# A graph attention layer on one core: target loads cut in 96 and 15 rows, weights moved to the second node pass, gather buffers from five to six

## The chip, the core and the metric

The kernel runs on one core of one Trainium2 chip. The metric is the time of one execution on the device, in microseconds (us). The core has five engines that run their own instruction streams and wait for each other by semaphores: TensorE (PE in the profile, with PEld for its weight loads), VectorE (DVE), ScalarE (ACT), GpSimd (POOL) and SyncE (SP). SP issues most transfers, ScalarE a few, and POOL the indirect ones, which gather or scatter rows by a list of indices. Each of these queues issues in order.

## The reference

One layer of attention over a graph with N = 12500 nodes of 128 channels and E = 400000 edges, sorted by target node (`dst`).

```python
h = maximum(layernorm(x), 0)
msg_src, msg_dst = h @ w_src + b_src, h @ w_dst          # per node
m = (msg_src[src] + msg_dst[dst]) * edge_weight * mlp(edge_attr)   # per edge; mlp 32-64-64-128, silu
m = m @ w_sep + b_sep                                    # 8 heads of 16 alphas and 16 values
score = sum(leaky(alpha) * alpha_dot)                    # leaky: a smooth leaky relu
att = softmax of score over the edges of one target
out = x + segment_sum(value * att, dst) @ w_proj + b_proj
```

## The kernel before

**Node passes** (in `gnn_kernel`, lines 171 to 618). The 98 blocks of up to 128 nodes go in 25 quads of four. The first pass (loop at line 575) does for each quad i: transposes of the normalized quad i + 1 and their relu (`turn`), the scaling of quad i + 3 on ScalarE and VectorE (`norm`), the product with w_src (`products(i, 0)`), whose result ScalarE copies to one of six buffers `ms0` and SP stores to the table `t_src` in memory, and the statistics of quad i + 5 (`stats`, `roots`, `scales`). The second pass (line 605) multiplies the same quads, kept in SBUF, with w_dst and stores pairs of quads to `t_dst` through four buffers `ms1`. It also normalizes 40 tiles of raw rows that POOL gathered for the first five steps (`raw_norm`, `raw_turn`), and runs a list of single jobs (`extra`).

Beside the passes lies work on the sorted targets. `load_targets` brings dst into the tile `cur`, 112 rows of seven sections of 512 edges; 111 rows are full and are loaded at once, the last one alone, and single words fill the columns at both sides. `load_limits` brings single words that are compared with thresholds. `sections` takes the first and last target of each section, `falls` and `fits` test whether the input has the expected shape and set `bad`, which decides a branch ahead of `windows`. `fits` ends with the stores of the sections' borders to memory (`ends_d`) and loads them back in three layouts (`eb`, `base`, `to`). In the first pass SP also issues the 29 loads of small weights and four of edge attributes, two a quad from quad 3 on (`weights_list`). `marks`, `spans`, `cuts`, `places`, `direct_ids` and `spreads` prepare, during the second pass, what the steps need; `cuts` and `places` alternate between TensorE and VectorE.

**Steps** (in `windows`, `step(k)`, line 1508). 391 steps of two sections (1024 edges) follow. Step k = 5 and later gather their source rows from `t_src` in eight indirect transfers of 128 rows (`gather`, line 1036), issued by POOL; steps 5 to 12 into the ring `messages`, later ones into the buffers `gs0` and `gs1`, one for each section of a step, GSB = 5 of each. TensorE turns them (`sources`, line 1096), adds the target rows (`message`, line 1108), VectorE multiplies with the radial network's result (`radial`, line 1085, which takes the edge weights from `w_b`). Then come alphas, scores, the softmax over eight steps at once (`softmax_*`), and, LAG = 12 steps later, values and sums. SP's order in a step is written out: stores of the window sums, `load_w(k + 2)` (512 KB, edge weights sent to all partitions, three buffers), `load_md(k + 4)` (rows of `t_dst`), every second step `load_d` (targets, `d_b`), then the later stores.

**Tail.** After the last step POOL loads rows of x into gather buffers (`big["xw"]`, `big["xe"]`) and the finished block rows from `obs_d` into two of the `w_b` buffers (`big["ye"]`), adds them (`sum_rows`) and scatters them to the output.

The pool `node` (h, ms0, ms1) is opened ahead of `node1` (x_all, cur, eb and others); the pools of `windows` take the same space afterwards, `lp` (loads) from its right end and `sp` (work tiles) from its left.

Of the kernel before, what the change touches and what calls it, by code (L numbers as in the profile page):

```python
# [21 lines left out]
P = 128  # L22
C = 128
# [28 lines left out]
GSB = 5  # L52
# [3 lines left out]
def gnn_kernel(ctx: ExitStack, tc: tile.TileContext, a: dict, out: bass.AP):  # L56
# [45 lines left out]
    groups = [(max(t, 0), min(t + XG, NF)) for t in range(4 - XG, NF, XG)]  # L102
# [69 lines left out]
    with tc.tile_pool(name="node", bufs=2) as np_, tc.tile_pool(name="node1", bufs=1) as n1, \  # L172
# [6 lines left out]
        nc.scalar.dma_start(out=w_dst, in_=a["w_dst"])  # L179
# [17 lines left out]
        assert 96 <= CP - 1 < P and 0 < CL < CC  # L197
        ones_b = n1.tile([P, 1], BF16, name="ones_b")
# [49 lines left out]
        def weights_list():  # L248

            pairs = []  # L250
            for name, t in wt.items():
# [149 lines left out]
        def fits():  # L401
# [11 lines left out]
            for n, o0, o1 in ((CP, 0, CL), (CP - 1, CL, CC)):  # L413
                for o in range(o0, o1, BANK):
# [18 lines left out]
            nc.vector.tensor_copy(bad, sum_)  # L433
            e0 = 1 + 2 * (CP - 1) * SPP
            nc.sync.dma_start(out=ends_d[:, 1:e0].rearrange("o (p c) -> (o p) c", p=CP - 1),
                              in_=ends[0:CP - 1].rearrange("p s i -> p (s i)"))
# [5 lines left out]
            nc.sync.dma_start(out=t_dst[N:N + W, :], in_=bare[:W, 0:C])  # L442
            nc.sync.dma_start(out=eb.rearrange("p s i -> p (s i)"),
# [20 lines left out]

        def places():

            on = n1.tile([NC, P], F32, name="on")
            nc.vector.tensor_tensor(on, to[:, 0, :], to[:, 1, :], op=ALU.is_equal)
            nc.vector.scalar_tensor_tensor(on, on, SKIP, to[:, 0, :], op0=ALU.mult, op1=ALU.add)
            pt = nps.tile([P, NC], F32, name="pb", bufs=1)  # L470
            nc.tensor.transpose(pt, on, ident[:NC, :NC])
            nc.vector.tensor_copy(ids, pt)
# [62 lines left out]
        def marks(j):  # L535
            s_ = slice(j * CC // 4, (j + 1) * CC // 4)
            nc.vector.tensor_tensor(sm[:, s_], cur[:, s_], cur[:, s_.start + 1:s_.stop + 1], op=ALU.not_equal)
            if j == 3:
                h = (CP - 1) * CC
                nc.sync.dma_start(out=same[:, 0:h].rearrange("o (p c) -> (o p) c", c=CC), in_=sm[0:CP - 1, :])  # L540
# [25 lines left out]
        for i in range(2, 5):  # L566
            stats(*quads[i])
            if i == 2:
                roots(*quads[i])
                scales(*quads[i])  # L570
                norm(i)
        ready = quads[3][0], quads[4][1]
        roots(*ready)
        more = iter(weights_list())
        for i in range(Q):
            if i + 1 < Q:
                turn(i + 1)
            if ready:
                scales(*ready)
                ready = None  # L580
# [3 lines left out]
            if i + 5 < Q:  # L584
                stats(*quads[i + 5])
            if i % 2 and i + 4 < Q:
                ready = quads[i + 4][0], quads[min(i + 5, Q - 1)][1]
                roots(*ready)
            if i == 1:
                load_targets()  # L590
                load_limits()
            if i >= 3:
                for load in (next(more, None), next(more, None)):
                    if load:
                        load()
# [8 lines left out]
        assert 2 * RQ + 1 < Q  # L604
        for i in range(Q):
            if i % 2 and 0 <= i // 2 - 1 < RQ:
                raw_turn(i // 2 - 1)
            products(i, 1)
            if i % 4 == 0 and i // 2 < RQ:
                raw_roots(i // 2, i // 2 + 2)  # L610
# [4 lines left out]
            if i in extra:  # L615
                extra[i]()
            if i == 2 * RQ - 2:
# [313 lines left out]
    def windows():  # L931
# [7 lines left out]
        with tc.tile_pool(name="ps", bufs=1, space=PSUM) as pp, \  # L939
# [68 lines left out]
            def load_w(k):  # L1008
                w_g[k] = lp.tile([P, PR], F32, name="w_b", bufs=3)
# [481 lines left out]
            def ye_at(g):  # L1491
                return big["ye", g // 8][:, g % 8 * C:(g % 8 + 1) * C]
# [10 lines left out]
            load_d(0)  # L1503
            for k in range(2):
                load_md(k)
                load_w(k)

            def step(k):
# [10 lines left out]
                if has(k + 2) and k >= 0:  # L1519
                    load_w(k + 2)  # L1520
# [138 lines left out]
            g0 = min(8, last - 1)  # L1659
            nc.gpsimd.dma_start(out=big["ye", 0][:, 0:g0 * C].rearrange("p (g c) -> p g c", c=C),  # L1660
                                in_=obs_d[0:g0 * P, :].rearrange("(g p) c -> p g c", p=P))
# [205 lines left out]
```

## Time and profile before

| | before |
|---|---|
| median of 3 runs | 4101.05 us (4093.68 to 4102.66) |
| profiled execution | 4092.9 us |
| its span | 4091.1 us |
| granted TensorE clock, mean | 0.987 |
| second node pass ends, steps begin | about 128 us |
| last gather of a step issued | 3988 us |

A page of the profile tells of one execution: busy time of each engine, the transfers, the chain of work that ended last, and the costliest groups of instructions by line. Views of the trace answer for a stretch of time, one line or one engine. In a row of the timeline stand start, duration, engine, line, operation, and in brackets the engine's idle time before it and what ended it. In a row of the waits stand the waiting line, what it waited for, the total, the count and the longest. In a row of busy time by stretch stand the stretch, then the busy time of PE, PEld, DVE, ACT and POOL with their counts (or of one line alone), the granted clock, the share of the DMA engines that was busy, and GB/s. "SPq" marks instructions of SP that issue transfers.

### The profile page before, as it was taken

How to read it: one execution, taken by the hardware profiler on the slowest of the kernel's cores; microseconds unless marked ns; L12 is line 12 of the kernel's file. 1: busy time of each engine (PE TensorE's matmuls, PEld its weight loads, DVE VectorE, ACT ScalarE, POOL GpSimd, SP SyncE). 2: the span in 40 equal slices, each digit the busy share in tenths (PEclk: the TensorE clock that was granted, in tenths of full speed). 3: DMA queues.
4: the chain of work that ended last, by engine and by line, in shares of the span. 5: the costliest groups of instructions: out<-in, count | busy, mean ns of one | idle time of the engine just before them, and what ended most of it. 6: DMA issues, size and time to landing. Idle time of an engine off the chain costs nothing.

```text
span 4091.1 us, 84238 instructions
## 1 busy us (share of the span) xinstructions
PE 3864.8 (94%) x27816; PEld 2340.9 (57%) x27816; DVE 3107.1 (76%) x5569; ACT 1880.1 (46%) x3824; POOL 3036.2 (74%) x3199
## 2 busy tenths in 40 slices
PE   6799999999999999999999999999999999999996
PEld 5455655655555555555555555555555555555555
DVE  6577777777777777777778777787777777777777
ACT  5454444444444444444444444444444444444441
POOL 4757777777777777777777777777777777777776
PEclk8899999999999999999999999999999999999998
DMA  6767777777767776776777676777776777767662
GB/s 212 216 172 196 195 179 194 195 179 194 197 185 178 193 192 170 190 196 182 179 191 195 190 188 188 187 184 192 200 194 177 192 199 193 189 187 196 187 174 56
DMA packets 534427, 762.19 MB, mean 186 GB/s; under 512 B 124496, under 2 KB 337522, under 8 KB 533871
## 3 DMA queue, kind: packets, MB, share of 16 engines
q1 hardware_dynamic: 375991, 498.26, 41.1%
q0 software_dynamic: 101872, 207.34, 23.3%
q10 hardware_dynamic: 56120, 51.10, 4.4%
q8 instruction: 226, 3.70, 0.4%
q14 instruction: 218, 1.79, 0.2%
HBM read 632.26 MB, written 125.70 MB: 185 GB/s over the span
## 4 chain that ended last, share of the span: by engine, by line
PE 62%; DMA 13%; POOL 10%; issue 7%; DVE 4%; ACT 2%; SPq 1%; ACTq 0%; DVEq 0%; POOLq 0%
PE V L1251 13%; PE pa L1119 12%; DMA gs<-t_src,idx 9%; POOL gs L1036 9%; PE misc L1264 7%; PE p L1080 6%; PE pm L1096 6%; PE m L1052 4%; PE pm L1108 4%; PE p L1065 3%; PE m L1136 3%; DVE mT L1113 1%; DMA agg<-ob 1%; DMA cur<-in_dst 1%; POOL mT L1036 0%
## 5 line engine op out<-in xcount | busy, mean ns | idle before, releaser
L1036 POOL DMA_INDIRECT gs<-t_src,idx x3021 | 2871.7, 951 | 942.1 <-issue 764.8
L1121 ACT ACTIVATE sl<-pa,c_b_a 128x512 f32<-128x512 f32 x782 | 537.4, 687 | 1087.8 <-PE pa L1119 1085.7
L1126 DVE SCALAR_TENSOR_TENSOR al<-pa,sl 128x512 f32<-128x512 f32 x782 | 537.6, 687 | 530.9 <-ACT sl L1121 522.6
L1251 PEld LDWEIGHTS V<-c_w_v,mT 128*128 128x128 f32 x6154 | 752.2, 192 | 304.8 <-DVE ob L1268 122.4
L1251 PE MATMUL V<-c_w_v,mT 128*128 128x128 f32 x6154 | 885.1, 287 | 2.8 <-DVE pvx L1253 2.7
L1119 PE MATMUL pa<-mT,c_w_a 128*128 128x512 f32 x1564 | 835.6, 616 | 25.0 <-DVE mT L1113 22.0
L1253 DVE TENSOR_TENSOR pvx<-V,Pem 128x512 f32<-128x512 f32 x770 | 529.2, 687 | 209.0 <-PE V L1251 190.7
L1067 ACT ACTIVATE h<-p,b 128x512 f32<-128x512 f32 x391 | 469.3, 1200 | 407.1 <-PE p L1065 328.8
L1096 PEld LDWEIGHTS pm<-ident,gs 128*128 128x128 f32 x3021 | 372.1, 141 | 483.7 <-issue 466.6
L1085 DVE SCALAR_TENSOR_TENSOR rad<-p,c_fc_b,w_b 128x1024 f32<-128x1024 f32 x391 | 501.1, 1281 | 108.0 <-PE p L1080 91.3
L1264 PEld LDWEIGHTS misc<-pvx,oh 128*64 128x64 f32 x6250 | 351.3, 137 | 292.2 <-ACT h L1055 281.9
L1096 PE MATMUL pm<-ident,gs 128*128 128x128 f32 x3021 | 456.4, 274 | 63.7 <-DMA gs<-t_src,idx 63.3
L1113 DVE SCALAR_TENSOR_TENSOR mT<-pm,c_b_src,rad 128x1024 f32<-128x1024 f32 x391 | 498.1, 1274 | 5.6 <-PE pm L1108 4.8
L1264 PE MATMUL misc<-pvx,oh 128*64 128x136 f32 x6250 | 450.9, 286 | 0.1
L1080 PE MATMUL p<-h,w3b 64*128 64x512 f32 x1564 | 405.1, 595 | 0.0
L1052 PE MATMUL m<-eT,w1b 64*128 64x256 f32 x782 | 275.7, 433 | 20.1 <-ACT qT L1346 14.2
L1108 PE MATMUL pm<-ohT,m 64*128 64x512 f32 x1564 | 286.7, 444 | 0.0
L1119 PEld LDWEIGHTS pa<-mT,c_w_a 128*128 128x128 f32 x1564 | 236.6, 191 | 75.5 <-DVE mT L1113 42.5
L1055 ACT ACTIVATE h<-misc,b 128x256 f32<-128x256 f32 x391 | 185.5, 474 | 201.5 <-PE misc L1052 184.1
L1052 PE MATMUL misc<-eT,w1b 64*128 64x256 f32 x782 | 275.8, 433 | 0.0
L1152 ACT ACTIVATE Sp<-m,b_s 128x512 f32<-128x512 f32 x192 | 131.7, 686 | 309.1 <-PE m L1136 306.8
L1065 PE MATMUL p<-h,w2b 64*64 64x256 f32 x3128 | 260.5, 403 | 2.7 <-DVE rad L1085 2.7
(217 smaller groups left out, 3552.5 us busy)
## 6 DMA issues: line engine op xcount, KB each, us to landing
w_b<-in_edge_weight SPq DMA_DIRECT2D x390, 512.0 KB
d_b<-in_dst SPq DMA_DIRECT2D x390, 256.0 KB
e_t<-in_edge_attr ACTq DMA_DIRECT2D x386, 128.0 KB
sc_d<-Sp SPq DMA_DIRECT2D x192, 256.0 KB
gs<-t_src,idx POOLq DMA_INDIRECT x3021
win<-ob SPq DMA_DIRECT2D x390, 68.0 KB
agg<-ob SPq DMA_DIRECT2D x762, 33.5 KB
md<-t_dst SPq DMA_DIRECT2D x782, 32.0 KB
```

The costliest lines, as they stand in the source:

```text
L1036: sent = [nc.gpsimd.indirect_dma_start(out=gs[:, t, :], out_offset=None, in_=t_src[:, :], in_offset=bass.IndirectOffsetOnAxis(ap=idx[:, t0 ...
L1052: nc.tensor.matmul(p1[f], w1b[s, :], eTs[k][s, :], start=True, stop=True)
L1080: nc.tensor.matmul(p3[:, f, 0:SEC], w3b[s, :], h2s[k][s, :], start=True, stop=True)
L1085: nc.vector.scalar_tensor_tensor(rad[:, 0:n], p3.rearrange("c f e -> c (f e)")[:, 0:n], b3, w_g[k][:, 0:n], op0=ALU.add, op1=ALU.mult)
L1096: turned = [nc.tensor.matmul(pm[:, t * T:(t + 1) * T], gs[:, t, :], ident, start=(t == 0), stop=False, is_transpose=True, skip_group_check ...
L1113: nc.vector.scalar_tensor_tensor(mTs[k][:, 0:n], pms.rearrange("c f e -> c (f e)")[:, 0:n], b_n, rad[:, 0:n], op0=ALU.add, op1=ALU.mult)
L1119: nc.tensor.matmul(pa[:, 0:n], w_a, mTs[k][:, f * SEC:f * SEC + n], start=True, stop=True)
L1121: nc.scalar.activation(sl[:, 0:n], pa[:, 0:n], AF.Silu, bias=b_a, scale=1.0)
L1126: nc.vector.scalar_tensor_tensor(al, pa, 0.25, sl, op0=ALU.mult, op1=ALU.add)
L1251: nc.tensor.matmul(V[:, t, :], mTs[c][:, o:o + T], w_v, start=True, stop=True)
L1253: nc.vector.tensor_mul(pvx[c][:, f, 0:n, 0:C].rearrange("p t (h k) -> p t h k", h=H), V[:, 0:n, :].rearrange("p t (h k) -> p t h k", h=H), ...
L1264: nc.tensor.matmul(acc[f * W:(f + 1) * W, :], ohs[c][:, f * TS + t, :], pvx[c][:, f, t, :], start=(t == 0), stop=(t == n - 1), skip_group_ ...
```

## The change

Nine edits:

1. Loads and stores of 111 rows are cut in rows 0 to 95 and 96 to 110 (`halves`): the targets, the stores of `ends` and of `same`. The targets are loaded after quad 3 rather than quad 1.
2. The x load of blocks 4 to 17 is cut in 4 to 7 and 8 to 17; w_dst is loaded by SP ahead of the first pass's loop rather than by ScalarE at the start.
3. In the first pass the square roots are taken at even quads and used at odd ones, and the statistics run six quads ahead.
4. Weights are loaded in the second pass, three a quad, those for `spans` and `cuts` first.
5. The stores of the borders stand between the passes (`ends_store`), their loads in quad 1 of the second (`ends_load`).
6. In the second pass `raw_turn` stands behind `products`, three quads behind its `raw_norm`; `cuts` does all its TensorE work first, in banks of its own, and `places` keeps only VectorE's part.
7. The pools `node` and `node1` are opened in the other order.
8. Six gather buffers of each kind (GSB), two of `w_b`: `load_w(k + 1)` in step k; the first loads are `load_md(0)`, `load_d(0)`, `load_w(0)`, `load_md(1)`, `load_w(1)`.
9. The tail's block rows lie in gather buffers, loaded in three parts rather than two.

```diff
-GSB = 5
+GSB = 6
...
-    groups = [(max(t, 0), min(t + XG, NF)) for t in range(4 - XG, NF, XG)]
+    groups = [(0, 4), (4, 8), (8, 18)] + [(t, min(t + XG, NF)) for t in range(18, NF, XG)]
...
-    with tc.tile_pool(name="node", bufs=2) as np_, tc.tile_pool(name="node1", bufs=1) as n1, \
+    with tc.tile_pool(name="node1", bufs=1) as n1, tc.tile_pool(name="node", bufs=2) as np_, \
...
-        nc.scalar.dma_start(out=w_dst, in_=a["w_dst"])
...
+        halves = [(0, 96), (96, CP - 1)]
...
-            nc.sync.dma_start(out=cur[0:h, 1:CC + 1], in_=dst[0:h * CC].rearrange("(p c) -> p c", c=CC))
+            for p0, p1 in halves:
+                nc.sync.dma_start(out=cur[p0:p1, 1:CC + 1], in_=dst[p0 * CC:p1 * CC].rearrange("(p c) -> p c", c=CC))
...
+            first = ("heads", "dot", "b_v", "w_proj", "b_proj", "b_a")
+            for name, t in sorted(wt.items(), key=lambda v: v[0] not in first):
...
+        def ends_store():
...
+            for p0, p1 in halves:
+                nc.sync.dma_start(out=ends_d[:, 1 + 2 * p0 * SPP:1 + 2 * p1 * SPP]
...
+        def ends_load():
...
         def cuts():
-            pv = nps.tile([P, 4, P], F32, name="pt")
-            nc.tensor.matmul(pv[:, 0, :], bvb, w_proj, start=True, stop=True)
-            nc.vector.tensor_add(b_out, pv[:, 0, :], b_out)
-            nc.tensor.transpose(pv[:, 1, :], bvb, ident)
-            nc.vector.tensor_scalar(bare[:, 0:C], pv[:, 1, :], -1e-16, None, op0=ALU.mult)
+            po = nps.tile([P, 4, P], F32, name="pt")[:, 0, :]
+            pr = nps.tile([P, 4, P], F32, name="pt")[:, 0, :]
             pb = nps.tile([P, 1], F32, name="pb", bufs=1)
+            pi = nps.tile([P, NC], F32, name="tot", bufs=1)
+            nc.tensor.matmul(po, bvb, w_proj, start=True, stop=True)
+            nc.tensor.transpose(pr, bvb, ident)
             for j in range(4):
                 nc.tensor.matmul(pb[32 * j:32 * j + 32, :], w_all, b_a, start=True, stop=True)
+            nc.tensor.transpose(pi, on, ident[:NC, :NC])
+            nc.vector.tensor_add(b_out, po, b_out)
+            nc.vector.tensor_scalar(bare[:, 0:C], pr, -1e-16, None, op0=ALU.mult)
             nc.vector.tensor_scalar(b_s, pb, 0.25, None, op0=ALU.mult)
-            places()
+            nc.vector.tensor_copy(ids, pi)
...
+        stats(*quads[3])
+        stats(*quads[4])
+        roots(quads[3][0], quads[4][1])
+        nc.sync.dma_start(out=w_dst, in_=a["w_dst"])
         for i in range(Q):
             if i + 1 < Q:
                 turn(i + 1)
-            if ready:
-                scales(*ready)
-                ready = None
+            if i == 0:
+                scales(quads[3][0], quads[4][1])
             if i + 3 < Q:
                 norm(i + 3)
             products(i, 0)
-            if i + 5 < Q:
-                stats(*quads[i + 5])
-            if i % 2 and i + 4 < Q:
-                ready = quads[i + 4][0], quads[min(i + 5, Q - 1)][1]
-                roots(*ready)
-            if i == 1:
+            for j in (5, 6) if i == 0 else (i + 6,):
+                if j < Q:
+                    stats(*quads[j])
+            j = i - i % 2 + 5
+            if j < Q:
+                (scales if i % 2 else roots)(quads[j][0], quads[min(j + 1, Q - 1)][1])
+            if i == 3:
                 load_targets()
                 load_limits()
-            if i >= 3:
-                for load in (next(more, None), next(more, None)):
...
-        extra = {2: lambda: marks(0), 4: lambda: marks(1), 6: lambda: marks(2), 8: lambda: marks(3),
-                 10: spans, 13: cuts, 15: direct_ids, 17: spreads}
+        extra = {1: ends_load, 2: lambda: marks(0), 4: lambda: marks(1), 6: lambda: marks(2), 8: lambda: marks(3),
+                 12: lambda: (spans(), places()), 14: cuts, 16: direct_ids, 18: spreads}
+        ends_store()
         for i in range(Q):
-            if i % 2 and 0 <= i // 2 - 1 < RQ:
-                raw_turn(i // 2 - 1)
             products(i, 1)
+            if i % 2 == 0 and 0 <= i // 2 - 2 < RQ:
+                raw_turn(i // 2 - 2)
...
+            for load in (next(more, None), next(more, None), next(more, None)):
+                if load:
+                    load()
...
-                w_g[k] = lp.tile([P, PR], F32, name="w_b", bufs=3)
+                w_g[k] = lp.tile([P, PR], F32, name="w_b", bufs=2)
...
-            load_d(0)
             for k in range(2):
                 load_md(k)
+                if k == 0:
+                    load_d(0)
                 load_w(k)
...
-                if has(k + 2) and k >= 0:
-                    load_w(k + 2)
+                if has(k + 1) and k >= 1:
+                    load_w(k + 1)
...
-            for i in range(2):
-                big["ye", i] = lp.tile([P, PR], F32, name="w_b", bufs=3)
+            for i in range(-(-NC // TS)):
+                big["ye", i] = lp.tile([P, TS, C], F32, name=f"gs{i % 2}", bufs=GSB)
...
+            for g in range(0, last - 1, TS):
+                n = min(TS, last - 1 - g)
+                nc.gpsimd.dma_start(out=big["ye", g // TS][:, 0:n, :],
+                                    in_=obs_d[g * P:(g + n) * P, :].rearrange("(g p) c -> p g c", p=P))
```

More of the change, by code (lines that the diff above doesn't have):

```diff
@@ L433, in fits @@
             nc.vector.tensor_copy(bad, sum_)
+        def ends_store():
             e0 = 1 + 2 * (CP - 1) * SPP
[L435 to L436 removed]
+            for p0, p1 in halves:
+                nc.sync.dma_start(out=ends_d[:, 1 + 2 * p0 * SPP:1 + 2 * p1 * SPP]
+                                  .rearrange("o (p c) -> (o p) c", c=2 * SPP),
+                                  in_=ends[p0:p1].rearrange("p s i -> p (s i)"))
             nc.sync.dma_start(out=ends_d[:, e0:2 * NS + 1], in_=ends[CP - 1:CP, 0:SL, :].rearrange("p s i -> p (s i)"))
@@ L539, in marks @@
                 h = (CP - 1) * CC
-                nc.sync.dma_start(out=same[:, 0:h].rearrange("o (p c) -> (o p) c", c=CC), in_=sm[0:CP - 1, :])
+                for p0, p1 in halves:
+                    nc.sync.dma_start(out=same[:, p0 * CC:p1 * CC].rearrange("o (p c) -> (o p) c", c=CC),
+                                      in_=sm[p0:p1, :])
                 nc.sync.dma_start(out=same[:, h:E], in_=sm[CP - 1:CP, 0:CL])
@@ L565, in gnn_kernel @@
             raw_gather(t)
[L566 to L572, printed above, removed]
-        roots(*ready)
-        more = iter(weights_list())
+        stats(*quads[2])
+        roots(*quads[2])
+        scales(*quads[2])
+        norm(2)
+        stats(*quads[3])
+        stats(*quads[4])
+        roots(quads[3][0], quads[4][1])
+        nc.sync.dma_start(out=w_dst, in_=a["w_dst"])
         for i in range(Q):
```

21 lines of the change are left out of this document (5 added, 16 removed).

## The prediction, made before the result

> **What bounds the kernel now.** I read the page first, then the gathers (the timeline of POOL, and busy time by stretch for two lines), and last the opening 160 us. TensorE's busy share is no proof of a bound, since another engine stands beside it all the way:
>
> ```profile
> span 4091.1 us, 84238 instructions
> PE 3864.8 (94%) x27816; PEld 2340.9 (57%) x27816; DVE 3107.1 (76%) x5569; ACT 1880.1 (46%) x3824; POOL 3036.2 (74%) x3199
> ...
> L1036 POOL DMA_INDIRECT gs<-t_src,idx x3021 | 2871.7, 951 | 942.1 <-issue 764.8
> ```
>
> The timeline of POOL has the first gather, the one long gap, and the last gather (columns: start, duration, what ended the idle time before):
>
> ```profile
> 95.37 0.94 POOL L1036 DMA_INDIRECT mT<-t_src,idx  x1 [32.39 <-DVE shiftr L363]
> ...
> 246.39 0.94 POOL L1036 DMA_INDIRECT gs<-t_src,idx  x1 [20.56 <-PE pm L1096]
> ...
> 257.33 0.94 POOL L1036 DMA_INDIRECT gs<-t_src,idx  x1 [0.30 <-DMA gs<-t_src,idx]
> ...
> 3988.46 0.94 POOL L1036 DMA_INDIRECT gs<-t_src,idx  x1 [0.30 <-issue]
> ```
>
> There are 64 + 3021 = 3085 gathers. From the first to the last are 3893.1 us; without the gap of 20.56 us that is 1.256 us for each of 3084, or 10.05 us for the eight of a step. POOL hardly rests elsewhere. Two stretches tell whether TensorE keeps ahead (L1036 gathers, eight a step; L1108 matmuls, four a step):
>
> ```profile
> 300.00:1200.00 900.00, 681.46 (x718) 1.00 0.72 190
> 1400.00:3400.00 2000.00, 1514.69 (x1593) 1.00 0.71 189
> ...
> 300.00:1200.00 900.00, 68.16 (x372) 27.68 (x372) 1.00 0.72 190
> 1400.00:3400.00 2000.00, 145.87 (x796) 59.25 (x796) 1.00 0.71 189
> ...
> PE pm L1096 <- DMA gs<-t_src,idx: 63.3, 65, 2.9
> ```
>
> Early, TensorE does 372/4 = 93 steps in 900 us (9.68 us each) while POOL does 718/8 = 89.8 (10.03): it eats up the lead that the gathers had. Later both do 199 in 2000 us, and over the whole run TensorE waits 63.3 us for gathers. So **the chain of gathers sets the end**. Time is gained only if gathers run earlier, up to TensorE's slack of 63.3 us. Steps 5 to 12 are gathered into the message ring and 13 to 17 into the five buffers, so the first gather of step 18, at 246.39, waits for TensorE to turn step 13 and free its buffer. **How early TensorE reaches step 13 sets everything behind it**, and that is the length of the node passes. There one hole stands out:
>
> ```profile
> 20.00:35.90 15.90, 13.66 (x89) 9.98 (x87) 12.41 (x35) 12.75 (x32) 12.07 (x13) 1.00 0.42 138
> 35.90:52.80 16.90, 0.25 (x3) 0.06 (x1) 0.84 (x3) 1.02 (x3) 12.80 (x14) 0.59 0.40 132
> 52.80:58.00 5.20, 4.59 (x17) 3.30 (x18) 3.31 (x9) 4.67 (x13) 4.17 (x4) 0.50 0.75 244
> 58.00:64.20 6.20, 6.20 (x36) 6.13 (x36) 6.17 (x14) 4.39 (x12) 3.87 (x4) 0.62 0.72 225
> ...
> L325 ACT COPY ms<-pm 128x512 f32<-128x512 f32 x1 | 0.6, 586 | 17.1 <-DMA t_src<-ms 17.1
> ...
> 22.37 25.27 SPq L241 DMA_DIRECT2D lim<-in_dst  x4
> ...
> q1 hardware_dynamic: 103, 1.48, 16.4%
> ```
>
> For 17 us TensorE does 0.25 us of work (first engine column). ScalarE waits for a t_src store; the store stands on SP behind the `lim` loads, whose issue takes 25 us; and those stand behind the targets, 111 rows of 14 KB. From 24 to 46 us SP's queue keeps 16.4% of 16 DMA engines busy, which is 2.6.
>
> **The change part by part.**
> *Targets in 96 and 15 rows.* A load of 128 rows shows what a good split does (2 to 10 us, x):
>
> ```profile
> q1 hardware_dynamic: 655, 2.83, 91.8%
> ...
> 30.77 1.06 PE L319 MATMUL pm<-w_src,x_all 128*128 128x128 f32 x8
> ...
> 34.99 1.16 PE L319 MATMUL pm<-w_src,x_all 128*128 128x128 f32 x8
> 54.23 1.92 PE L319 MATMUL pm<-w_src,x_all 128*128 128x128 f32 x8
> ```
>
> That is 14.7 engines; at its 2.83 MB in 8 us the targets' 1.59 MB (111 rows of 14 KB) take 4.5 us, against some 25 now. Quads of blocks come every 2.1 us (two of them in 34.99 - 30.77 = 4.22); across the hole one takes 19.24. So 17.1 us go, and they go whole, as 4.5 us are covered by the six t_src buffers (six quads, 12.7 us). The load now stands behind the stores of quads 2 and 3 on SP and starts some 4 us later in the pass; the section ends are read in quad 9, twelve us on, so that stays covered too. If it weren't, VectorE would wait there and with it the relus, a microsecond for a microsecond. After the hole eight matmuls take 1.92 us instead of 1.06, at a clock of 0.50 and then 0.62: over three quads that is 2.6 us, of which I take 1.5, as ScalarE is as busy there (4.67 of 5.20 us). [...]
>
> *First x load cut in two.* VectorE waits for it:
>
> ```profile
> 8.59 0.76 DVE L277 BATCH_NORM_STATS2 mv<-x_all 128x6 f32<-128x256 f32 x2 [2.32 <-DMA x_all<-in_x]
> ...
> 64.20:84.20 20.00, 16.94 (x118) 12.77 (x117) 15.87 (x54) 15.41 (x39) 0.00 (x0) 1.00 0.42 143
> 84.20:128.00 43.80, 36.14 (x250) 30.78 (x248) 28.27 (x91) 28.54 (x66) 24.91 (x26) 0.92 0.69 239
> ...
> 107.50:111.00 3.50, 1.38 (x15) 0.98 (x15) 2.52 (x10) 2.09 (x5) 2.59 (x4) 0.92 0.80 281
> ```
>
> The second quad's blocks no longer come with ten more, so that wait goes: 2.3 us gained (bounds 2.3 and, for one more issue, a loss of 0.4).
> *Roots and scales a quad apart.* VectorE no longer stops behind ScalarE's square roots. TensorE idles 2.2 of 15.9 us before the hole and 3.1 of 20 late in the pass; over the pass's 50 us without the hole that bounds the gain by 0 and 7. I take 2.0, since ScalarE's row (15.41 of 20) leaves little less room than TensorE's.
> First pass: 2.3 + 17.1 + 1.5 + 2.0 = **22.9 us** earlier.
>
> *Second pass.* It lasts from 84.2 to 128, and TensorE idles 7.7 us of it. `cuts` without its back and forth between TensorE and VectorE frees the 2.1 idle us of its stretch (last row); raw rows turned behind the products rather than ahead of them, and a start that finds the t_src stores done, free part of the other 5.6. I take 4.0 of 7.7. Against it stands SP, which now issues here what it issued in the first pass:
>
> ```profile
> 57.47 0.46 SPq L266 DMA_DIRECT2D c_w_a<-in_w_a  x1
> ...
> 75.76 4.23 SPq L460 DMA_DIRECT2D to<-ends_d  x1
> ...
> 90.18 0.75 SPq L335 DMA_DIRECT2D t_src<-ms  x1
> ...
> 128.59 0.84 SPq L335 DMA_DIRECT2D t_dst<-ms  x1
> 129.70 1.34 SPq L1004 DMA_DIRECT2D d_b<-in_dst  x2
> 131.90 0.77 DVE L1045 STREAM_TRANSPOSE eT<-e_t 128x256 f32<-128x256 f32 x2 [6.74 <-DMA t_dst<-ms]
> 132.39 0.79 PE L1052 MATMUL m<-eT,w1b 64*128 64x256 f32 x1 [4.92 <-DVE eT L1045]
> 132.55 1.24 SPq L1018 DMA_DIRECT2D md<-t_dst  x2
> ```
>
> 33 weight and edge loads at some 0.5 us are 16.5 us; borders, node numbers and marks some 10 (one issue alone is 4.23 us, behind a list of single words); 14 t_dst stores some 7. SP has time for these 34 in 40 us, but not early: reading the borders back waits for their stores to land, with three loads and the first t_dst stores queued behind it, and then three loads a quad are 1.5 us of issue where a quad takes 1.6. By quad 11 the stores run some 12 us late. The four t_dst buffers hold eight quads, 12.8 us, less the time that a store needs to land. I charge 3.0 us of ScalarE's waiting (bounds 0 and 10). The pass ends 1.0 us shorter.
> *Pools swapped, first loads reordered.* The first transpose takes its space from tiles that are read out by then, no longer from those that the last t_dst store reads, so TensorE's 4.92 us of waiting go. But the table rows (`md`) cannot land sooner, and the target rows (1.34 us of issue), until now issued under that wait, stand behind them, with all of SP's first loads. I take a loss of 0.5 us (bounds: a gain of 4.9, a loss of 2).
> TensorE reaches step 13 earlier by 22.9 + 1.0 - 0.5 = **23.4 us**.
>
> *Sixth buffer.* Step 19 waits for step 13 instead of step 18. Its first gather moves from 257.33 to where step 18's stands, **10.9 us**, if POOL is there by then. The gathers begin 5.2 us after the last t_src store's issue (95.37 - 90.18), and that issue no longer lags 6 us behind the pass (90.18 against 84.2), as SP's list has left it; I give it 1: 84.2 - 22.9 + 1 + 5.2 = 67.5. The 112 gathers of steps 5 to 18, at 1.256, end at 208.2, before 246.39 - 23.4 = 223.0. So POOL still waits some 15 us there, and an earlier t_src table brings nothing by itself; that wait is what is late next.
>
> *Two w_b buffers instead of three* are the price. A load takes the queue place of the load behind it:
>
> ```profile
> 2022.31 0.36 SPq L1011 DMA_DIRECT2D w_b<-in_edge_weight  x1
> ...
> 2036.03 1.28 DVE L1085 SCALAR_TENSOR_TENSOR rad<-p,c_fc_b,w_b 128x1024 f32<-128x1024 f32 x1
> ...
> 1074.64 6.45 DMA w_b<-in_edge_weight
> ...
> SPq L1210 <- DVE M L1178: 215.7, 48, 6.1
> ```
>
> The issue at 2022.31 serves the radial after the one at 2036.03 today, and would serve that one: 13.7 us ahead of it, against 6.45 for a landing, the longer of two that stand in the chain of waits. Behind the load on SP stand the table and target rows of later steps, which have as much time. I take nothing (bounds: nothing, and the last rival).
> *Tail.* The block rows take the gather buffers of the last two steps, turned before POOL is through with its 13 row loads; one more issue on POOL comes ahead of an idle time of 20 us:
>
> ```profile
> 4050.14 1.03 POOL L1305 DMA_INDIRECT out<-gs,ids_d  x1 [20.46 <-DVE dq L1285]
> ```
>
> So nothing there.
>
> **Sum.** 23.4 + 10.9 = 34.3 us. The profiled execution took 4092.9 us (span 4091.1): 4058.6. The median of the runs is 8.2 higher (4101.05, runs from 4093.68); I go half way, **4062.7, rounded 4062**.
>
> **The rivals.**
> *SP takes the hole's place* (15%): the second pass ends when SP has worked off its list, 7 to 12 us later than I have it. For it: 34 us of issues in some 40, and nothing early. Against it: 24 of them, the loads and borders, come in the first eleven quads, so that SP can catch up in the last fourteen. A gain of 34.3 - 9.5, so 4072.
> *More comes* (15%): SP's lateness costs nothing and the swap frees all 4.92 us; gain 34.3 + 3.0 + 5.4 = 42.7, under POOL's bound of 34.3 + 15. Then 4054. For it: a TensorE that runs ahead of `md` works off what it can; against it: `md` and its queue come late either way.
> *The split doesn't spread* (5%): both loads crawl, the hole stays, and 34.3 - 18.6 leaves 15.7: 4081. [...] The 2.6 engines speak against it.
> *Slower: late edge weights* (10%). SP stands behind the maxima's store 48 times (4.5 us each, last row), and a load queued one place later may then land after its radial needs it. TensorE's 63.3 us of slack less the 10.9 used absorb 52, the gain another 34: from 86 us of lateness, 1.8 us at each of the 48, it is slower. At 3 us each (144) it is 4062 + 92 = 4154; if it spreads to every step, more.
>
> **How the numbers follow.** My forecast has 55%, with 4056 to 4070 of its own. With the first two rivals 4048 to 4080 leaves out some 2 in 10. Within 0.2% (8 us, about what a measurement here can tell) I give 1%. Faster 89%, slower 10%.
>
> **What would show it.** Right: no 17 us hole before 60 us, the targets landed within 6 us of issue; the last t_dst store near 105; gathers restarting near 70, one gap of about 15 us before step 19 near 223, and the last gather near 3954. Wrong: ScalarE waiting long for t_dst stores in the second pass; the gap gone, or gathers unbroken at 1.255 us yet no earlier; radials waiting for w_b.

## The result and the profile after

| | before | changed |
|---|---|---|
| median of 6 runs | 4101.52 us (4093.68 to 4103.40) | 4068.55 us (4064.11 to 4070.95) |
| profiled execution | 4092.9 us | 4070.95 us |
| its span | 4091.1 us | 4069.2 us |

The ratio is 0.9922, 95% interval 0.9909 to 0.9935: faster by 33.0 us between the medians. The forecast was 4062, with 4048 to 4080 as its range. The two profiled executions lie only 21.9 us apart: that of before is faster than all six of its timed runs, that of the changed kernel is the slowest of its six. The third experiment returns to this difference.

The page of the changed kernel, its opening lines and the gathers:

```profile
span 4069.2 us, 84290 instructions
...
PE 3866.4 (95%) x27816; PEld 2351.1 (58%) x27816; DVE 3104.6 (76%) x5569; ACT 1873.5 (46%) x3824; POOL 3039.6 (75%) x3200
...
L1049 POOL DMA_INDIRECT gs<-t_src,idx x3021 | 2873.0, 951 | 940.1 <-issue 766.1
```

Busy time hardly moved, as it should where only waits go. The timeline of POOL has the first gather, the one long gap and the last gather:

```profile
70.39 0.94 POOL L1049 DMA_INDIRECT mT<-t_src,idx  x1 [7.59 <-DMA c_dot<-in_dot]
...
229.12 0.94 POOL L1049 DMA_INDIRECT gs<-t_src,idx  x1 [17.50 <-PE pm L1109]
...
3963.55 0.95 POOL L1049 DMA_INDIRECT gs<-t_src,idx  x1 [0.30 <-PE V L1264]
```

There is still one gap, 17.50 us, and by count it stands ahead of step 19 as forecast: 28.2 us earlier than step 19 stood before (257.33). The last gather is 24.9 us earlier.

Of TensorE's timeline, four rows: the first and the last product of the second pass, the first wait of the steps, and the message of step 13 (L1121 is L1108 of before, L321 is L319):

```profile
64.06 4.63 PE L321 MATMUL pm<-w_dst,x_all 128*128 128x128 f32 x40
...
111.01 2.76 PE L321 MATMUL pm<-w_dst,x_all 128*128 128x128 f32 x12
...
127.12 0.76 PE L1065 MATMUL m<-eT,w1b 64*128 64x256 f32 x1 [8.72 <-DVE eT L1058]
...
234.72 0.73 PE L1121 MATMUL pm<-ohT,m 64*128 64x512 f32 x4
```

The same rows of before, as far as they weren't shown:

```profile
84.22 2.84 PE L319 MATMUL pm<-w_dst,x_all 128*128 128x128 f32 x24
...
124.19 3.29 PE L319 MATMUL pm<-w_dst,x_all 128*128 128x128 f32 x28
...
252.00 0.73 PE L1108 MATMUL pm<-ohT,m 64*128 64x512 f32 x4
```

From these rows, and from the spans above, the account can be made term by term, forecast against profile (minus is earlier):

| step of the forecast | forecast, us | two profiles, us | from |
|---|---|---|---|
| first pass | -22.9 | -20.2 | 84.22 to 64.06 |
| second pass | -1.0 | +6.4 | 43.3 (to 127.48) against 49.7 (to 113.77) |
| opening of the steps, to step 13 | +0.5 | -3.6 | 124.5 against 120.9 |
| sixth buffer | -10.9 | -10.9 | 28.2 at step 19, less 17.3 at step 13 |
| gathers from step 19 to the last | 0 | +3.3 | 28.2 less 24.9 |
| from the last gather to the end | 0 | +3.0 | 102.6 against 105.6 |
| sum | -34.3 | -22.0 | |

The gain of the forecast (34.3 us) came close to that of the medians (33.0), but terms within it were off in both directions, and the two profiles show only 22.0. The experiments ask which of them are real.

### The profile page after: what moved, and what is told of

Read it like the earlier page. It is cut to its first block, busy times and chain, and to the rows that moved or that the text cites. A ratio compares the mean times of both kernels' runs of the same rounds, so it can differ in the third digit from the quotient of the medians.

```text
span 4069.2 us, 84290 instructions
## 1 busy us (share of the span) xinstructions
PE 3866.4 (95%) x27816; PEld 2351.1 (58%) x27816; DVE 3104.6 (76%) x5569; ACT 1873.5 (46%) x3824; POOL 3039.6 (75%) x3200
## 4 chain that ended last, share of the span: by engine, by line
PE 69%; DMA 10%; DVE 5%; POOL 5%; issue 5%; SPq 2%; ACT 2%; ACTq 0%; DVEq 0%; POOLq 0%
PE V L1264 15%; PE pa L1132 14%; PE misc L1277 8%; PE p L1093 7%; PE pm L1109 7%; DMA gs<-t_src,idx 6%; PE m L1065 5%; POOL gs L1049 5%; PE pm L1121 4%; PE p L1078 4%; PE m L1149 3%; DMA agg<-ob 2%; DVE mT L1126 2%; DMA win<-ob 1%; ACT sl L1134 1%
## 5 line engine op out<-in xcount | busy, mean ns | idle before, releaser
L1121 PE MATMUL pm<-ohT,m 64*128 64x512 f32 x1564 | 286.5, 444 | 0.0
L1248 DVE TENSOR_TENSOR oh<-lane,misc 128x504 f32<-128x504 f32 x391 | 261.4, 668 | 0.1
```

## The experiments

In two groups of runs every kernel, the one before included, took 5.3 ms instead of 4.1. These six (changed again, the first with the target rows first, ends read later, the first with the words ahead, and the two with late targets) have no time that settles anything about the node passes; what they do show stands with the last experiment and at the end. The reference for the others is the changed kernel's 4068.55. (Beside the second "target rows first" and the second "words ahead" the kernel before took 4097.27 instead of 4101.5, so 4 us between groups of runs say nothing.)

### Whole rows

```diff
-        halves = [(0, 96), (96, CP - 1)]
+        halves = [(0, CP - 1)]
```

> The changed kernel with its 111-row transfers whole again (targets, borders, section marks); all else as changed. Theory (the split spreads the load over the engines; gathers set the end, and they follow the step-13 time): the hole comes back. The section ends are read about 9 us after the load's issue and already wait 5.0 us for it with the split; a load at 2.6 engines lands some 28 us after its issue instead of 14, so VectorE waits some 14 us more, and the kernel takes 4068.6 + 14 = 4083 (4079 to 4088). Rival, two partition parts don't spread: no change, 4068.6 within 4. Rival, TensorE's own work sets the end rather than the gathers: under half, 4069 to 4075.

Measured: 4094.20 us, ratio to before 0.9986 (0.9977 to 0.9995). By the medians the split alone is worth 25.6 us, more than theory (14) and forecast (18.6); in the two profiles the first gather of step 19 is 19.3 us apart (229.12 against 248.42). The profiled execution of whole rows is the fastest of its eleven, that of the changed kernel the slowest of its six. Busy time by stretch, changed kernel first:

```profile
20.00:26.00 6.00, 5.77 (x41) 4.33 (x39) 5.61 (x16) 6.00 (x17) 4.48 (x6) 1.00 1.07 358
26.00:32.00 6.00, 5.72 (x39) 4.27 (x37) 4.45 (x14) 6.00 (x17) 4.48 (x6) 1.00 1.01 211
32.00:38.00 6.00, 1.46 (x6) 1.07 (x6) 1.69 (x7) 2.03 (x6) 3.42 (x4) 0.81 0.60 102
```

With whole rows:

```profile
26.00:32.00 6.00, 5.71 (x39) 4.28 (x37) 4.45 (x14) 6.00 (x17) 4.48 (x6) 1.00 0.33 114
...
38.00:44.00 6.00, 0.00 (x0) 0.00 (x0) 0.00 (x0) 0.00 (x0) 4.59 (x5) 0.50 0.35 118
```

In the last column but one, from 26 to 32 us all DMA engines are busy with the split load (1.01), a third of them with the whole one (0.33). With whole rows TensorE (busy time behind the length of the stretch) then stands still, as from 38 to 44 us. These engines carry other transfers too, POOL's gathers of raw rows among them. SP's queue alone, from 26 to 32 us, in packets, MB and share of the 16 engines, changed kernel first and then whole rows:

```profile
q1 hardware_dynamic: 92, 1.12, 86.8%
```

```profile
q1 hardware_dynamic: 30, 0.38, 15.9%
```

The split moves three times as much in the same 6 us. But it takes more than five times the engine time for it: 0.91 us of an engine for each packet (86.8% of 16 engines for 6 us, over 92), where whole rows take 0.51. This will matter below. The timeline of TensorE with whole rows shows that the hole comes back, and a second one with it:

```profile
50.40 2.08 PE L321 MATMUL pm<-w_src,x_all 128*128 128x128 f32 x8 [17.62 <-DVE x_all L312]
...
122.48 2.07 PE L321 MATMUL pm<-w_dst,x_all 128*128 128x128 f32 x8 [10.98 <-ACT ms L327]
```

The second hole was in nobody's account: it follows the whole store of the section marks (`same`), behind which two short issues on SP take 9.36 us, with t_dst stores behind them. (That the store is the cause is argued from the order of the rows and from the split, which is the only difference.)

```profile
105.67 0.26 SPq L555 DMA_DIRECT2D same<-past  x1
...
109.71 1.15 SPq L335 DMA_DIRECT2D t_dst<-ms  x1
110.90 9.36 SPq L268 DMA_DIRECT2D b<-in_fc_b  x2
```

Without the split, all other edits together bring 7.5 us (4101.65 to 4094.20), no more than the new buffers bring alone (8.7, below). The rival that a split in partitions brings nothing is refuted, as 15.9% against 86.8% of the 16 engines shows. Why 111 rows in one load keep so few engines busy, and whether 96 and 15 are the best parts, isn't shown: no other cut was run.

### Five buffers

```diff
-GSB = 6
+GSB = 5
...
-                w_g[k] = lp.tile([P, PR], F32, name="w_b", bufs=2)
+                w_g[k] = lp.tile([P, PR], F32, name="w_b", bufs=3)
...
-                if has(k + 1) and k >= 1:
-                    load_w(k + 1)
+                if has(k + 2) and k >= 0:
+                    load_w(k + 2)
```

The tail's block rows go back to the `w_b` tiles as well.

> The changed kernel with the old buffers: five gather buffers of each kind, three of the edge weights, block rows of the tail in the edge weights' buffers. Theory (chain of gathers): the first gather that must wait is step 18's again, which stands 10.9 us later in the chain: 4068.6 + 10.9 = 4079.5 (4076 to 4083), POOL's long wait stays near 17 us and is for step 18. Rival (TensorE bounds the later steps, gathers run ahead in vain): the same within 4 us.

Measured: 4082.87 us, ratio 0.9959 (0.9944 to 0.9974), 14.3 us more than the changed kernel. The first gather of steps 18 and 19:

```profile
228.92 0.95 POOL L1049 DMA_INDIRECT gs<-t_src,idx  x1 [27.55 <-PE pm L1109]
...
239.88 0.95 POOL L1049 DMA_INDIRECT gs<-t_src,idx  x1 [0.30 <-issue]
```

Step 18 takes the place that step 19 had, and step 19 is 10.8 us later (239.88 against 229.12), as worked out; only the length of the gap (27.55, expected 17) was set down wrong, since POOL comes there one step earlier. TensorE reaches step 13 at 234.53 in this profile, within 0.2 us of the changed kernel.

### Only the buffers

The same edit the other way, on the kernel before: GSB = 6, two `w_b`, tail's rows in gather buffers.

> The kernel before with only the new buffers (six gather buffers, two of the edge weights, tail's block rows in gather buffers). Theory: 10.9 us off, 4101.5 - 10.9 = 4090.6 (4087 to 4094); POOL's long wait falls from 20.6 to about 10. Rival, edge weights land late with two buffers: no gain, 4101 or more, with radials waiting for them. Rival, TensorE bounds: gain under 4 us.

Measured: 4092.94 us against 4101.65 for before beside it, ratio 0.9976 (0.9967 to 0.9985): 8.7 us faster, within the theory's range. Its profile holds something else. The first passes of this kernel and of before are the same program, and yet:

```profile
61.67 1.63 PE L308 MATMUL pt<-ident,h 128*128 128x128 f32 x4 [25.67 <-ACT h L296]
...
260.23 0.73 PE L1108 MATMUL pm<-ohT,m 64*128 64x512 f32 x4
```

The hole is 25.67 us long here, 16.66 in the profile of before, and step 13 comes at 260.23 instead of 252.00. The length of the hole belongs to the execution, not to the program, so the 17.1 us read from one profile can be too small for the median. That most runs of before have a long hole isn't shown, though, and the same profile holds a rival:

```profile
254.62 0.95 POOL L1036 DMA_INDIRECT gs<-t_src,idx  x1 [9.03 <-PE pm L1096]
...
4000.51 0.95 POOL L1036 DMA_INDIRECT gs<-t_src,idx  x1 [0.31 <-issue]
```

From step 19 to the last gather are 3745.9 us here, 3731.1 in the profile of before (257.33 to 3988.46). So this execution, the slowest of its eleven and 12.2 us above their median, loses 8.2 us by the hole and 14.8 by gathers that lie further apart. The profiles show 11 us less gain than the medians because that of before lies 8.6 us under its median and that of the changed kernel 2.4 above its own; whether the hole or the gathers make the 8.6, these runs don't tell.

### Weights first

```diff
+        more = iter(weights_list())
         for i in range(Q):
...
+            if i >= 4:
+                for load in (next(more, None), next(more, None)):
+                    if load:
+                        load()
...
-            for load in (next(more, None), next(more, None), next(more, None)):
-                if load:
-                    load()
```

> The changed kernel with the small weights and first edge attributes issued in the first pass again, two a quad from quad 4. Theory (SP's list holds up the t_dst stores of the second pass; ScalarE and TensorE wait there for 8.7 us in two waits): these two waits go, step 13 comes 6 to 9 us earlier, POOL's long wait of 17.5 us shrinks by as much, and the kernel takes 4060 to 4063. Rival (SP is then late with the t_src stores in the first pass): the first pass grows by as much, 4068 within 4. Rival (the borders' read-back alone, with its 6.3 us issue, causes it): under 3 us gained.

Measured: 4065.35 us, ratio 0.9915 (0.9902 to 0.9928): 3.2 us faster than the changed kernel, and the intervals overlap, so no difference that these runs can tell. TensorE:

```profile
64.27 4.63 PE L321 MATMUL pm<-w_dst,x_all 128*128 128x128 f32 x40
...
85.20 2.08 PE L321 MATMUL pm<-w_dst,x_all 128*128 128x128 f32 x8 [3.92 <-ACT ms L327]
...
101.76 1.50 PE L321 MATMUL pm<-w_dst,x_all 128*128 128x128 f32 x12
...
224.69 0.73 PE L1122 MATMUL pm<-ohT,m 64*128 64x512 f32 x4
```

and POOL:

```profile
219.09 0.95 POOL L1050 DMA_INDIRECT gs<-t_src,idx  x1 [2.81 <-PE pm L1110]
...
3960.15 0.95 POOL L1050 DMA_INDIRECT gs<-t_src,idx  x1 [0.30 <-issue]
```

As far as step 19 the theory holds to the letter: the first pass is no longer (64.27 against 64.06), the second ends at 103.3 instead of 113.8, step 13 and the gather of step 19 both come 10.0 us earlier, and POOL's wait shrinks to 2.81. What is left, 3.92 us, stands behind the read-back of the borders (by the order of the rows; it wasn't tried). But of these 10.0 us the last gather has only 3.4: from step 19 on, the gathers are 1.2588 us apart on average, against 1.2565 in the profile of the changed kernel, which over 2972 of them is the missing 6.6. POOL waits for nothing there in either (from 300 us on no wait is longer than 1.0 us); the gathers themselves take longer, as will be seen below. The rival of a TensorE that holds the gathers back is not what the rows show; over this run TensorE still waits 58.8 us for gathers.

### Target rows first

```diff
+            load_d(0)
             for k in range(2):
                 load_md(k)
-                if k == 0:
-                    load_d(0)
                 load_w(k)
```

> The changed kernel with the first target rows (d_b) loaded ahead of the first table rows (md), as in the kernel before. Theory (TensorE's wait of 8.7 us at the start of the steps ends with d_b, which lands 4.3 us after the table rows were worked off, because it stands behind them on SP): step 0 comes 4.3 us earlier, step 13 and the gather of step 19 too, 4068.6 - 4.3 = 4064 (4062 to 4066). Rival (the wait is the table rows' own, which wait for the last t_dst store): step 13 within 1 us, 4068.6 within 3.

That run took 5325.80 (before 5333.60, ratio 0.9985, 0.9965 to 1.0006). The edit was run again:

> The changed kernel with the first target rows (d_b) loaded ahead of the first table rows (md), once more, as all kernels of the last call took 5.3 ms. Theory (TensorE's wait of 8.7 us at the start of the steps ends with d_b, 4.3 us after the table rows were worked off): step 0 at 127.4 instead of 131.7, step 13 at 230.4 instead of 234.7, the gather of step 19 at 224.8 instead of 229.1; 4064 (4062 to 4066). Rival (the wait is the table rows' own, for the last t_dst store): step 13 within 1 us, 4068.6 within 3.

Measured: 4067.84 us, ratio 0.9932 (0.9919 to 0.9946), nothing gained. The first wait of the steps is shorter, and two steps later all is as it was:

```profile
125.25 0.76 PE L1065 MATMUL m<-eT,w1b 64*128 64x256 f32 x1 [4.39 <-DVE eT L1058]
...
146.70 0.73 PE L1121 MATMUL pm<-ohT,m 64*128 64x512 f32 x4
...
234.88 0.74 PE L1121 MATMUL pm<-ohT,m 64*128 64x512 f32 x4
```

Step 2 is at 146.70, against 146.56 in the changed kernel. The waits from 130 to 148 us name the reason, which the changed kernel doesn't have there: SP's next rows are late in turn.

```profile
DVE ohT L1087 <- DMA d_b<-in_dst: 3.1, 1, 3.1
```

My theory falls: the order of the first loads decides which step waits, not when step 13 comes.

### Ends read later, words ahead

```diff
-            if i == 9:
+            if i == 13:
                 sections()
-            if 10 <= i < 14:
-                falls(i - 10)
-            if i == 15:
+            if 14 <= i < 18:
+                falls(i - 14)
+            if i == 19:
                 fits()
```

> The changed kernel with the section ends read in quad 13 instead of 9, and what follows on them four quads later. Theory A (what is left of the hole is VectorE's wait of 5.0 us for the targets, with 1.9 us of cold clock behind it): the first pass is 5 to 7 us shorter, 4062 to 4064. Theory B (SP, held for 10 us by the issue of the single words, stores no t_src rows from 22 to 37 us either, and six buffers hold no more than 11 us): ScalarE waits for t_src stores in its place, at most 2 us gained.

This took 5321.15 (0.9984, 0.9965 to 1.0004). "Words ahead" adds `load_limits()` ahead of the loop in place of behind `load_targets()`:

> As the run with the section ends read later, and the single words for the limits (lim) issued before the loop, ahead of the targets rather than behind them. Theory B (the single words' issue holds SP because they queue behind the targets' rows): SP is free by 24 us, no hole is left, the first pass is 6 us shorter than the changed kernel's, 4062 to 4063. Theory A: no more than reading the ends later brings by itself, and SP is then held by another issue behind the targets.

That took 5315.17 (0.9978, 0.9957 to 1.0000), and again:

> The changed kernel with the section ends read in quad 13 instead of 9 and the single words for the limits (lim) issued before the loop, ahead of the targets. Theory (what is left of the hole is VectorE's 5.0 us for the targets with 1.9 us of cold clock, and SP, held for 10 us by the single words behind the targets' rows): no hole is left, TensorE's second pass starts at 58 instead of 64, 4062 to 4063. Rival (the targets' rows hold whatever SP issues behind them, so the t_src stores are held instead of the single words, and ScalarE waits for them): second pass at 62 to 64, 4066 to 4069.

Measured: 4067.76 us, ratio 0.9936 (0.9922 to 0.9950), nothing gained. TensorE and, below, the waits from 16 to 66 us:

```profile
42.81 1.46 PE L310 MATMUL pt<-ident,h 128*128 128x128 f32 x4 [6.51 <-ACT h L298]
...
67.02 3.18 PE L321 MATMUL pm<-w_dst,x_all 128*128 128x128 f32 x27
```

```profile
ACT ms L327 <- DMA t_src<-ms: 7.4, 2, 6.7
```

VectorE no longer waits for the targets, and the hole is still there, under another name: ScalarE waits 6.7 us for a t_src store. SP begins the next t_src store 0.1 us behind the targets' loads, but this one issue takes 5.64 us, where 25 of them in the changed kernel have a median of 0.32:

```profile
29.34 5.64 SPq L335 DMA_DIRECT2D t_src<-ms  x1
```

The rival holds in its wait and in its time: the targets' rows hold what SP issues behind them, here this store for 5.64 us, in the changed kernel the single words for 10.13 (four issues of `lim`). (The second pass starts later than it had it, at 67.02 instead of 62 to 64, in an execution 6.7 us above the median.) What is left of the hole is the targets' own transfer and what waits behind it.

### Targets late

My reading at this point was that the DMA engines have no room from 20 to 32 us (1.07 and 1.01 in the changed kernel's rows), and that the targets should be loaded when the x loads are through: after quad 9, with the ends read in quad 17.

> The changed kernel with the targets and the limits' words loaded after quad 9 instead of 3, and the section ends and what follows eight quads later. Theory C (the split spreads the targets, but the DMA engines are then full from 8 to 32 us, with the x loads, the stores and the raw rows, so that the t_src stores land late and ScalarE waits; from 44 us on they are busy for 67%): behind the x loads the targets find room, the waits of 4.4 us and the 1.9 us of cold clock go, the second pass starts at 58 to 59 instead of 64, step 13 comes 5 us earlier, 4063 (4061 to 4065). Rival (not the load but the place on SP: targets and single words hold the t_src stores wherever they stand): the hole moves to quads 10 to 13, second pass at 63 to 65, 4067 to 4070.

> As the run with the targets late, and the small weights in the first pass again. Theory C with the weights' 10 us at step 13: step 13 at 219 to 220, gathers of step 19 bound by the t_src table alone (POOL's gap under 4 us), which is ready 5 us earlier than with the weights alone; 4065.4 - 5 = 4060 (4057 to 4062). Rival (TensorE bounds the later steps, and what is gained at step 13 is lost again): 4065 within 2.

Measured: 5337.97 (ratio 1.0002, 0.9983 to 1.0020) and 5328.67 (0.9990, 0.9975 to 1.0004), against 5335.25 for before. Both took 5.3 ms, as before did beside them, and neither has a time that speaks for or against theory C. But the profile of the first shows the targets' transfer behind the x loads, from 80 to 84 us, when no other queue moves anything:

```profile
q1 hardware_dynamic: 76, 1.02, 107.3%
```

That is 0.90 us of an engine for each packet, as in the changed kernel from 26 to 32 us (0.91). Room left by other loads doesn't make the targets' rows faster, as far as an execution of 5.3 ms can tell, and this speaks against theory C. It stays open whether a version with late targets and weights in the first pass beats the changed kernel; none that ran at 4.1 ms does so beyond its interval.

## Why the prediction was right, and where it was not

**The bound.** Right. One gap of POOL ahead of step 19, gathers without a break behind it, and the two runs with the buffers moved show that what moves the buffers moves the end; whole rows shows the same for step 13. In weights first, step 13 moved 10.0 us and the last gather 3.4, the rest lost to the gathers' pace.

**Targets in 96 and 15 rows, and the first pass.** Right in mechanism. The forecast gave the split 18.6 us (17.1 and 1.5); by the medians it is worth 25.6, by the two profiles 19.3 at step 19, and part of that is the second hole, which the forecast did not see (that the `same` store causes it is argued above). The two small terms of this pass (2.3 and 2.0 us) came as forecast up to the hole: its eleventh product starts at 30.51 instead of 34.99, 4.5 us earlier.

```profile
30.51 1.06 PE L321 MATMUL pm<-w_src,x_all 128*128 128x128 f32 x8
```

Of the 20.2 us by which this pass ends earlier, this leaves 15.7 to the hole, where 18.6 were forecast. "Landed within 6 us of issue" failed: the load was issued at 22.10 and the ends, read in quad 9, had to wait for it until 36.31.

```profile
36.31 0.26 DVE L227 COPY ends<-cur 112x7 int32<-112x7 int32 x2 [5.02 <-DMA cur<-in_dst]
```

The failing step is the 4.5 us, an estimate that gave parts of 96 and 15 rows the rate of the x load's 128 rows (2.83 MB in 8 us). Until 26 us the engines also work off what was issued earlier (1.07 busy, 358 GB/s). But from 26 to 32 us SP's queue moves only 1.12 MB while it keeps 86.8% of the engines busy: 0.19 MB a us, against 0.35 for x. (Some 80 packets of this stretch are over 8 KB, as only the targets' rows of 14 KB are among SP's loads here, so nearly all of it is targets.) A MB of x took 42 us of engine time (91.8% of 16 engines for 8 us), a MB here takes 74. At 0.19 MB a us the targets' 1.59 MB would take some 8.5 us, an estimate. Why these rows take so much more engine time with all engines at them than with two or three isn't shown. The late landing costs 4.43 us of TensorE and a slower clock once more (the granted clock is 0.50 from 36 to 42 us), more than the 2.7 us that the first pass fell short of 22.9:

```profile
37.21 2.08 PE L321 MATMUL pm<-w_src,x_all 128*128 128x128 f32 x8 [4.43 <-DVE x_all L312]
...
102.39 1.16 PE L321 MATMUL pm<-w_dst,x_all 128*128 128x128 f32 x8 [2.27 <-ACT ms L327]
```

After a wait of 4.43 us eight matmuls take 2.08 us, at a granted clock of 0.50 (37.2 to 39.3 us); after one of 2.27 they take 1.16, at 1.00 (102 to 104 us).

**Second pass.** Wrong: forecast 1.0 us shorter, measured 6.4 longer, and the sign of being wrong that the forecast named, ScalarE waiting long for t_dst stores, is there. The failing step is "I charge 3.0 us of ScalarE's waiting (bounds 0 and 10)". From 66 to 140 us ScalarE waits four times for t_dst stores, and TensorE for ScalarE:

```profile
ACT ms L327 <- DMA t_dst<-ms: 15.9, 4, 6.6
...
PEld pm L321 <- ACT ms L327: 9.4, 3, 6.0
```

Taking the weights out shortens the pass by 10.7 us (from 49.7 to 39.0), so the charge should have been 10.7 us, just above its upper bound, and the rival "SP takes the hole's place" had it right for this term. The argument against it, that SP can catch up in the last fourteen quads, doesn't help: SP does catch up, but what ScalarE has waited by then isn't won back.

**Pools swapped, loads reordered.** Forecast +0.5, measured -3.6, within the bounds. Target rows first shows that the order of md and d_b has no part in it; which of the other edits does wasn't tried.

**Sixth buffer.** Right: 10.9 in the profile, 8.7 and 14.3 us by the two pairs of runs.

**Two w_b buffers.** Right, at nothing. One radial in 391 waits for its weights (its idle time, by what ended it):

```profile
  DMA w_b<-in_edge_weight: 0.6, 1
```

The rival of late edge weights, the forecast's only loss, is refuted.

**Behind step 19.** The forecast had nothing there. The profiles show 3.3 and 3.0 us against the change. The first lies in the gathers' average distance (1.2565 us against 1.2554), not in the commonest one, which is the same in both (below). Of the tail's 3.0 it stays open whether they belong to the change: from the last gather to the end of the span, the old tail takes 102.6 us (before) and 96.3 (five buffers), the new one 102.9 (only the buffers) to 105.6 (changed). It wasn't tried by itself.

The median came out 6.5 us above the forecast, inside its own range of 4056 to 4070. That it came so near is in part luck. In the profiles the change is 12.3 us short of the 34.3, with terms that miss both ways: the first pass (2.7), the second (7.4) and what follows step 19 (6.3) against 4.1 gained in the opening. Of the 12.3, the half way to the median of before that the forecast allowed takes up 4.1, and 2.4 go because the changed kernel's profiled execution lies that much above its median. (The sum, 4062.7, rounds to 4063 and not 4062; nothing hangs on it.) What makes most executions of before longer than the one that was read, the hole or the gathers' pace, is open.

## What to carry to other kernels

Before a wait is priced from one profile, ask whether its length belongs to the program: a wait on a slow transfer differed by 9 us between two executions of one opening. A transfer that leaves most engines idle (here 111 rows, at 15.9% of 16) can be worth splitting even for a 15-row rest (86.8%, and 25.6 us by the medians); but don't price its landing from another load's rate: here a packet took 0.91 us of an engine with all engines at the rows, and 0.51 with two or three. And when work is moved out of one pass, count the issue queue of the pass that receives it quad by quad; a queue that has time on average can still be late where the buffers are few.

## What the runs showed of the hardware

The pace of the gathers is not one number. The group of all gathers takes 951 ns for one on the page of the changed kernel (shown above). On the pages of five buffers and of only the buffers it is longer:

```profile
L1049 POOL DMA_INDIRECT gs<-t_src,idx x3021 | 2883.0, 954 | 949.9 <-issue 771.3
```

```profile
L1036 POOL DMA_INDIRECT gs<-t_src,idx x3021 | 2885.1, 955 | 931.3 <-issue 770.0
```

The commonest distance of two gathers is 1.249 us in the profiles of before, changed, whole rows, target rows first and words ahead, and 1.252 in those of five buffers, only the buffers and weights first: 3 ns, and 9 us over 3000 gathers, as much as the sixth buffer. Whole rows, five buffers, only the buffers and weights first ran on one chip, one after the other, and show both. The changed kernel itself had 1.249 in its run at 4.1 ms and 1.252 in the one at 5.3; so it isn't the program alone, but what sets it stays open.

The changed kernel again:

> The changed kernel itself once more, as the measure for the three beside it and for the pace of the gathers. In the three profiles of before, of the changed kernel and of whole rows, the commonest distance of two gathers was 1.249 us; in the profiles of five buffers, of only the buffers, and of weights first it was 1.252, which is 9 us over 3000 gathers. If the pace belongs to the execution, this profile may show either; if it belongs to the program, it shows 1.249 again. Time: 4068.6 within 3.

It took 5325.28 us against 5333.60 (ratio 0.9986, 0.9965 to 1.0007). A wider stretch of that profile and its costliest waits in the steps:

```profile
300.00:5100.00 4800.00, 3928.77 (x25835) 2319.81 (x25835) 2830.81 (x4967) 1689.67 (x3453) 2807.51 (x2949) 0.93 0.55 146
```

```profile
POOL gs L1049 <- PE pm L1109: 756.2, 284, 59.5
POOL gs L1049 <- issue: 717.2, 2299, 1.3
ACT sl L1134 <- PE pa L1132: 527.7, 220, 6.1
```

The DMA engines are less busy than in the stretches shown of before (0.55 against 0.71), so they aren't what is full. POOL waits 756 us for TensorE, so the gathers are no longer the bound, and a change that starts them earlier is worth nothing there. Two chips ran this way; the cause can't be seen in these profiles.
